# Regrouping VectorE's column copies into loads of 20, 20, 24 and 12 numbers, with destinations fetched for two chunks at a time

## The chip, the cores and the metric

The kernel runs on one core of one Trainium2 chip. The metric is device time in microseconds (us) of one launch; the lower the better. The core has five engines with a queue of instructions each: TensorE (PE, with weight loads shown apart as PEld), VectorE (DVE), ScalarE (ACT), GpSimd (POOL) and SyncE (SP). SP computes nothing here: it loads numbers into registers and issues DMA transfers.

## The reference

One layer of a graph network with 12500 nodes of 48 features and 400000 edges, sorted by destination:

```python
h = jnp.maximum(_layernorm(x, axis=-1), 0.0)
x_i, x_j = h[dst], h[src]
tmp = jnp.concatenate([x_i, x_j, edge_attr], axis=1)   # 48 + 48 + 32
msg = jax.nn.relu(tmp @ W1 + b1) @ W2 + b2             # 128 hidden, then 48
out = x + jax.ops.segment_sum(msg, dst, num_segments=12500)
```

## The kernel before

**Tables.** A first stage of some 100 us (`node_tables`) normalises the nodes and multiplies them by the two node parts of W1. It leaves `tab_a` (for destinations) and `tab_b` (for sources) in HBM, one row of 128 numbers a node, and `bt`, which is `tab_b` turned: 128 partitions by nodes, in SBUF.

**Chunks and tiles.** The stage in question (`windows`) runs over 391 chunks of 1024 edges, each of 8 tiles of 128 edges. Because edges are sorted, the destinations of a chunk lie in a window of 80 nodes. For chunk c:

- SP loads the window's 80 rows of `tab_a` into `rhs` (L474), the edge features into the lower rows of `lhs` (L479), and the chunk's destinations as 16-bit numbers, repeated over 80 partitions, into `row` (L481).
- DVE compares `row` with the window's node numbers and writes the upper 80 rows of `lhs` (L501), and makes `hot`, the same comparison turned (L508).
- PE multiplies `lhs` and `rhs` tile by tile into `pre` in PSUM (`before`, L520). What the sources add comes in one of three ways, below.
- DVE adds `pre` and the fetched rows with the ReLU into `hid` (`gathered`, L540). PE folds `hid` with `hot` into `p_g` (`fold`, L567 and L572), and DVE adds that into the segment being summed (`add`, L586).

**Three ways for the sources.** The rows of `tab_b` for the sources of a tile are

- fetched by POOL with an indirect DMA (L490), 2619 tiles of the 3125;
- or copied column by column out of `bt` into a tile `gt` and added on PE by a product with the identity (`turned`, L530): 458 tiles. Each column is one copy with a register as its address, made by DVE or ACT (`columns`, L431);
- or brought by SP, one line of 512 bytes a DMA (`singles`, L462): 48 tiles, into the buffers `gbs`.

**What sets the order.** The order is written out by hand. The table `PARTS` says how many columns an engine copies at each place in a chunk. Ahead of each group stands one register load of as many numbers (`numbers`, L396, TENSOR_LOAD in the trace); DVE's first group loads one number more, the place used by `add`. Of the 151 columns of a chunk DVE copies 71 and ACT 80. DVE's program of a chunk is: the comparison L501, a load of 24 and 23 copies, `hot` L508, a load of 20 and 20 copies, the sum L540, a load of 20 and 20 copies, the addition L586, a load of 8 and 8 copies. `BYCOLS` spreads the tiles that are copied by columns evenly over the chunks by the total `PART`; `BYROWS` does the same for the tiles that SP brings, by `SINGLE` lines a chunk.

SP's program of a chunk is: a load of one number (the window), three transfers, a load of 16 numbers, 16 lines. `row` has three buffers, `lhs` and `rhs` three each. POOL's fetches for a chunk are issued about seven chunks ahead, each behind a DVE instruction that `paced` chooses, so that they are spread over a chunk.

Of the kernel before, what the change touches and what calls it, by code (L numbers as in the profile page):

```python
# [17 lines left out]
P = 128  # L18
N, D, DE, HID, E = 12500, 48, 32, 128, 400000
# [5 lines left out]
CE = T * P  # L25
# [3 lines left out]
W = 80  # L29
# [18 lines left out]
I16 = mybir.dt.int16  # L48
# [8 lines left out]


PARTS = (
    (True, 0, 23, 1),  # L60
    (True, 23, 20, 24),
    (True, 43, 20, 44),
    (True, 63, 8, 64),
    (False, 71, 16, 72),
    (False, 87, 16, 88),
    (False, 103, 16, 104),
    (False, 119, 16, 120),
    (False, 135, 16, 136),
)
PART = sum(n for _, _, n, _ in PARTS)  # L70
BASE = 152
DVE_PARTS = sum(dve for dve, *_ in PARTS)

BT0 = 16512
SEG0 = 133024
SEG_SIZE = 8 * L


SEG, NEXT, SEG2 = 153, 154, 155
PLACE0 = 156  # L80
SINGLE = 16
SINGLE_AT = 160
WIDTH = 176
SLOTS = (NCH + 2 + P - 1) // P
MOST = 32
HALF_ROWS = 16
# [10 lines left out]
def tiles_of(first, part):  # L97

    n = (END - first) * part // P
    return [first + (P * (j + 1) + part - 1) // part - 1 for j in range(n)]  # L100
# [14 lines left out]
def single_tiles():  # L115

    chunks = []
    for c in tiles_of(COLS, SINGLE):
        c = max(c, chunks[-1] + 1 if chunks else 0)
# [10 lines left out]
def single_at(c):  # L130

    return (0,) if c in BYROWS else ()


def gathered_at(c):

    return [
        t for t in range(min(T, NT - c * T)) if t not in turned_at(c) and t not in single_at(c)
    ]
# [155 lines left out]
def windows(nc, tc, gbs, bt, ident, idx, x_t, tab_a, tab_b, dst, edge_t, w1, w2s, b2s, out_t):  # L295
# [3 lines left out]
    with ExitStack() as es:  # L299
# [1 line left out]

        segs = [seg.tile([P, 2, L], F32, name=f"seg{k}") for k in range(2)]
        one = es.enter_context(tc.tile_pool(name="wone", bufs=1))
        ld = es.enter_context(tc.tile_pool(name="ld", bufs=LOADS))
        gtp = es.enter_context(tc.tile_pool(name="gtp", bufs=8))
        wp = es.enter_context(tc.tile_pool(name="wp", bufs=HIDS))
        ps_p = es.enter_context(tc.tile_pool(name="ps_p", bufs=2, space=PSUM))
# [13 lines left out]
        for _, _, n, at in PARTS:  # L321
# [3 lines left out]
            )  # L325
        rows_at = slice(BASE, BASE + 1)
        singles_at = slice(SINGLE_AT, SINGLE_AT + SINGLE)
        for of in (rows_at, singles_at):
# [5 lines left out]
        for a, b in ((place, SEG2), (NEXT, SEG)):  # L334
# [5 lines left out]
        nc.vector.scalar_tensor_tensor(  # L340
            last[:, :, at_place], last[:, :, at_place], 4.0, last[:, :, PLACE0 : PLACE0 + 1],
            op0=ALU.mult, op1=ALU.add,
# [6 lines left out]
        def after(ins, of, reason):  # L349
            tc.add_manual_dep(  # L350
                ins, of.name,
                mybir.DependencyInfo(
                    mybir.DependencyClass.Sync, mybir.DependencyReason.DATA
                ),
                reason=reason,
            )
# [11 lines left out]
        def buffer(c):  # L368

            if c in BYROWS:  # L370
                return mixed[BYROWS.index(c) % 2]
            k = 0 if len(turned_at(c)) == 1 else 1
            uses[k] += 1
            return gbs[k][(uses[k] - 1) % len(gbs[k])]
# [9 lines left out]
        def group(c):  # L384

            return divmod(c + OFF, GQ)
# [4 lines left out]
        def numbers(c, at, n, engine):  # L391

            got = []
            row, slot = row_of(c)
            for k in range(0, n, MOST):
                got += nc.values_load_multi_w_load_instructions(  # L396
                    last[row : row + 1, slot, at + k : at + min(k + MOST, n)],
                    engines=[engine], min_val=0, max_val=1 << 23,
                    skip_runtime_bounds_check_because="numbers of nodes, and what is made of them",
                )[1]  # L400
            return got
# [6 lines left out]
        def load(c, part):  # L408

            dve, first, n, at = PARTS[part]  # L410
            n = max(0, min(n, len(BYCOLS) * P - ((c - COLS) * PART + first))) if c >= COLS else 0
            engine = mybir.EngineType.DVE if dve else mybir.EngineType.Activation
            if part == 0 and 2 <= c < NCH + 2:
                base, *nodes = numbers(c, at - 1, n + 1, engine)
                st[c - 2]["base"] = base
            else:
                nodes = numbers(c, at, n, engine) if n else []
            regs[c, part] = nodes

        def columns(c, part):  # L420

            dve, first, _, _ = PARTS[part]
            copy = nc.vector.tensor_copy if dve else nc.scalar.copy
            for k, at in enumerate(regs.pop((c, part), [])):
                of, e = divmod((c - COLS) * PART + first + k, P)
                if of not in gts:
                    gts[of] = gtp.tile([HID, P], F32, name="gt")
                at = at.with_bounds(
                    min_val=BT0, max_val=BT0 + 4 * (N - 1), guaranteed_mod_val=0, out_of_modulus=4
                ) - BT0  # L430
                done = copy(gts[of][:, e : e + 1], bt8[:, bass.ds(at, 4)].bitcast(F32))  # L431
                if dve:
                    mark(done, 0.06)
# [4 lines left out]
        def mark(ins, us):  # L438
            marks.append((ins, us))

        def paced(c, j, of):

            span = spans.get(c - AHEAD + 1)
            if j == 0 or not span:
                return None
            upto = sum(us for _, us in span) * j / of
            for ins, us in span:
                upto -= us
                if upto <= 0:
                    return ins  # L450
            return None
# [3 lines left out]
        def singles(c):  # L455

            n = max(0, min(SINGLE, len(BYROWS) * P - (c - COLS) * SINGLE)) if c >= COLS else 0
            for k, row in enumerate(numbers(c, SINGLE_AT, n, mybir.EngineType.SP) if n else ()):
                of, e = divmod((c - COLS) * SINGLE + k, P)
                to = mixed[of % 2][:, single_at(BYROWS[of])[0], :]  # L460
# [4 lines left out]
                )  # L465
                moves.setdefault(BYROWS[of], []).append(moved.ins)

        def prepare(c):
            n = min(T, NT - c * T)
            at = c * CE  # L470
            base, = numbers(c, BASE, 1, mybir.EngineType.SP)
            rhs = rhss[c % 3]
            base = base.with_bounds(min_val=0, max_val=4 * HID * (N - 1))
            nc.sync.dma_start(  # L474
                rhs.bitcast(U8)[:W, :],
                taba8[bass.ds(base, 4 * HID * W)].rearrange("(w h) -> w h", w=W),
            )
            lhs = lhss[c % LOADS]
            nc.sync.dma_start(lhs[W:K, : n * P], edge_t[:, at : at + n * P])  # L479
            row = ld.tile([W, CE], I16, name="row")  # L480
            nc.sync.dma_start(  # L481
                row[:, : n * P],
                dst[at : at + n * P].rearrange("(o e) -> o e", o=1).to_broadcast([W, n * P]),
            )
            st[c] = dict(n=n)
            gb = buffer(c)
            fetched = gathered_at(c)
            fetches = []
            for j, t in enumerate(fetched):
                fetch = nc.gpsimd.indirect_dma_start(  # L490
                    out=gb[:, t, :], out_offset=None, in_=tab_b[:, :],
                    in_offset=bass.IndirectOffsetOnAxis(
                        ap=srci[:, c * T + t : c * T + t + 1], axis=0
                    ),
                )
                fetches.append(fetch.ins)
                behind = paced(c, j, len(fetched))
                if behind is not None:
                    after(fetch.ins, behind.ins, "fetches are spread over a chunk")

            mark(nc.vector.tensor_tensor(  # L501
                lhs[:W, : n * P], row[:, : n * P],
                firsts[:, c : c + 1].to_broadcast([W, n * P]), op=ALU.is_equal,
            ), 1.1)
            load(c, 0)
            columns(c, 0)
            hot = wp.tile([P, T, W], F32, name="hot")
            mark(nc.vector.tensor_tensor(  # L508
                hot[:, :n, :], wnum.unsqueeze(1).to_broadcast([P, n, W]),
                rel[:, c * T : c * T + n].unsqueeze(2).to_broadcast([P, n, W]), op=ALU.is_equal,  # L510
            ), 0.85)
            st[c].update(rhs=rhs, lhs=lhs, gb=gb, hot=hot, fetches=fetches)
# [64 lines left out]
        def add(c):  # L577

            s = st.pop(c)
            k = group(c)[0] % 2  # L580
            of = SEG0 + k * SEG_SIZE
            at = s["base"].with_bounds(
# [45 lines left out]
        with tc.manual_schedule():  # L628
            for c in range(NCH + 2):
                if c < NCH:  # L630
                    prepare(c)
                    singles(c)
# [173 lines left out]
def tile_gnn_preln(  # L806
# [52 lines left out]
    flag = const.tile([1, 1], I32, name="flag")  # L859
    last = const.tile([P, LAST, WIDTH], I32, name="last")  # L860

# [167 lines left out]
```

## Time and profile before

| | |
|---|---|
| median of 3 runs | 3493.72 us (3492.07 to 3495.51) |
| the profiled execution: time | 3493.84 us |
| the profiled execution: span from first to last instruction | 3492.1 us |
| busy: DVE, ACT | 3136.6 us (90%), 3172.3 us (91%) |
| busy: PE, POOL | 2656.1 us (76%), 2493.5 us (71%) |
| granted TensorE clock | 0.776 |
| DMA | 98 GB/s over the span |

Busy time of an engine counts its computing instructions alone: register loads and the issue of DMAs aren't in it, so SP has no busy share at all, and a gap on DVE may be a register load. In the rows below, "[idle before <-releaser]" is the time an engine stood still just before the row and what ended it; "issue" means nothing that the trace shows. SPq and DVEq are the sequencers of SP and DVE.

### The profile page before, as it was taken

The page shows a single profiled execution, that of the slowest core. Times are in us where ns is not written, and L with a number is a line of the kernel's source. Part 1 is how long each engine was busy: PE and PEld are TensorE (multiplying, and loading weights), DVE is VectorE, ACT ScalarE, POOL GpSimd, SP SyncE. Part 2 cuts the span into 40 slices and gives each one's busy share as a digit, 9 for nine tenths or more (in the row PEclk, how much of TensorE's full clock was granted, in tenths as well). Part 3 has the DMA queues.
Part 4 walks back from the last instruction along what each step waited for, and adds up shares of the span by engine and source line. Part 5 has one row for each costly group of instructions (what it writes and reads, how often), then busy time and mean ns, then how long its engine had stood idle before and what let it go on. Part 6 is the DMA issues. An engine that isn't in the chain of part 4 may idle for free.

```text
span 3492.1 us, 121785 instructions
## 1 busy us (share of the span) xinstructions
PE 2656.1 (76%) x17111; PEld 2384.2 (68%) x17111; DVE 3136.6 (90%) x29346; ACT 3172.3 (91%) x31179; POOL 2493.5 (71%) x2656
## 2 busy tenths in 40 slices
PE   8577777777778777777777777777778777777777
PEld 6566666666667667676676677666677676667666
DVE  6799999999999999999999999999999999999997
ACT  5999999998999999998999899999999899989893
POOL 5777777777777777777777777777777777777772
PEclk9777777877777777778777777778777777777777
DMA  5533333333333333333333333333333333333332
GB/s 196 168 98 97 95 97 94 97 98 100 96 96 98 96 96 97 95 97 100 96 97 97 97 95 97 95 98 98 98 96 96 97 95 97 97 96 97 96 99 56
DMA packets 199941, 349.44 MB, mean 100 GB/s; under 512 B 69106, under 2 KB 107396, under 8 KB 197844
## 3 DMA queue, kind: packets, MB, share of 16 engines
q0 software_dynamic: 83840, 171.83, 19.4%
q1 hardware_dynamic: 115024, 169.63, 16.1%
q14 instruction: 672, 5.51, 0.5%
q8 instruction: 145, 2.38, 0.3%
q10 hardware_dynamic: 260, 0.10, 0.0%
HBM read 321.82 MB, written 22.07 MB: 98 GB/s over the span
## 4 chain that ended last, share of the span: by engine, by line
DVE 49%; SPq 16%; PE 9%; ACT 9%; DMA 7%; issue 7%; DVEq 3%; ACTq 1%
DVE gt L431 27%; SPq L462 9%; ACT gt L431 8%; DVE lhs L501 8%; DVE hid L540 7%; DMA row<-in_dst 6%; DVE hot L508 5%; SPq L396 4%; DVEq L396 3%; PE p_g L567 3%; PE pre L520 2%; DVE seg L586 1%; PE p_n L241 1%; SPq L479 1%; SPq L474 1%
## 5 line engine op out<-in xcount | busy, mean ns | idle before, releaser
L431 ACT COPY gt<-bt 128x1 f32 x31040 | 3069.6, 187 | 70.0 <-issue 48.2
L490 POOL DMA_INDIRECT gb<-tab_b,srci x1855 | 1750.1, 943 | 669.2 <-issue 379.6
L431 DVE COPY gt<-bt 128x1 f32 x27584 | 1815.8, 144 | 208.9 <-issue 166.4
L567 PE MATMUL p_g<-hot,hid 128*128 128x80 f32 x6250 | 1075.9, 344 | 695.8 <-DVE hid L540 681.4
L567 PEld LDWEIGHTS p_g<-hot,hid 128*128 128x128 f32 x6250 | 1008.4, 253 | 766.6 <-DVE hid L540 751.1
L520 PEld LDWEIGHTS pre<-rhs,lhs 112*128 112x128 f32 x6250 | 974.1, 245 | 199.6 <-issue 127.9
L520 PE MATMUL pre<-rhs,lhs 112*128 112x128 f32 x6250 | 1013.7, 330 | 111.9 <-PE pre L530 48.7
L490 POOL DMA_INDIRECT gbl<-tab_b,srci x476 | 448.9, 943 | 165.6 <-issue 97.9
L501 DVE TENSOR_TENSOR lhs<-row,compared 80x1024 f32<-80x1024 int16 x391 | 472.5, 1209 | 73.7 <-DMA row<-in_dst 71.9
L490 POOL DMA_INDIRECT gbs<-tab_b,srci x288 | 271.7, 943 | 93.6 <-issue 59.8
L540 DVE CUSTOM_DVE_ANT_0 hid<-pre,gb 128x1024 f32<-128x1024 f32 x275 | 333.3, 1212 | 3.6 <-PE pre L530 3.0
L508 DVE TENSOR_TENSOR hot<-compared,rel 128x640 f32<-128x640 f32 x391 | 318.1, 813 | 0.0
L530 PE MATMUL pre<-ident,gt 128*128 128x128 f32 x916 | 274.8, 408 | 5.3 <-issue 4.8
L572 PE MATMUL p_g<-hot,ones 128*128 128x80 bf16 x3125 | 241.9, 239 | 0.0
L572 PEld LDWEIGHTS <-ones 128*128 128x128 bf16 x3125 | 241.8, 133 | 0.0
L530 PEld LDWEIGHTS pre<-ident,gt 128*128 128x128 f32 x916 | 195.9, 273 | 7.4 <-issue 6.1
L600 ACT COPY seg<-nothing 128x944 f32<-128x944 f32 x64 | 62.4, 975 | 151.1 <-PE p_f L616 151.1
L586 DVE TENSOR_TENSOR seg<-seg,p_g 128x160 f32 x391 | 121.2, 310 | 2.2 <-PE p_g L572 2.2
L616 PE MATMUL p_f<-seg,w2s 128*48 128x512 f32 (+1 forms) x134 | 96.4, 812 | 0.8 <-DVE xseg L622 0.8
L540 DVE CUSTOM_DVE_ANT_0 hid<-pre,gbl 128x1024 f32<-128x1024 f32 x68 | 82.6, 1214 | 3.7 <-PE pre L530 3.6
L617 PE MATMUL p_f<-seg,b2s 1*48 1x512 f32 (+1 forms) x134 | 81.5, 691 | 0.0
L617 PEld LDWEIGHTS p_f<-seg,b2s 1*48 1x48 f32 x134 | 11.9, 130 | 78.4 <-issue 77.0
(74 smaller groups left out, 391.4 us busy)
## 6 DMA issues: line engine op xcount, KB each, us to landing
gbs<-tab_b SPq DMA_DIRECT2D x6144, 0.5 KB
row<-in_dst SPq DMA_DIRECT2D x390, 160.0 KB
lhs<-in_edge_t SPq DMA_DIRECT2D x390, 128.0 KB
gb<-tab_b,srci POOLq DMA_INDIRECT x1855
rhs<-tab_a SPq DMA_DIRECT2D x391, 40.0 KB
gbl<-tab_b,srci POOLq DMA_INDIRECT x476
xseg<-in_x_t SPq DMA_DIRECT2D x33, 192.0 KB
out_x<-xseg SPq DMA_DIRECT2D x33, 192.0 KB
```

Of the source, the lines that this page charges most:

```text
L396: got += nc.values_load_multi_w_load_instructions(last[row : row + 1, slot, at + k : at + min(k + MOST, n)], engines=[engine], min_val=0, ...
L431: done = copy(gts[of][:, e : e + 1], bt8[:, bass.ds(at, 4)].bitcast(F32))
L462: moved = nc.sync.dma_start(to.bitcast(U8)[e : e + 1, :], tabb8[bass.ds(row, 4 * HID)].rearrange("(o h) -> o h", o=1),)
L490: fetch = nc.gpsimd.indirect_dma_start(out=gb[:, t, :], out_offset=None, in_=tab_b[:, :], in_offset=bass.IndirectOffsetOnAxis(ap=srci[:, c ...
L501: mark(nc.vector.tensor_tensor(lhs[:W, : n * P], row[:, : n * P], firsts[:, c : c + 1].to_broadcast([W, n * P]), op=ALU.is_equal,), 1.1)
L508: mark(nc.vector.tensor_tensor(hot[:, :n, :], wnum.unsqueeze(1).to_broadcast([P, n, W]), rel[:, c * T : c * T + n].unsqueeze(2).to_broadca ...
L520: s["behind"] = nc.tensor.matmul(pre[:, t, :], s["lhs"][:K, t * P : (t + 1) * P], s["rhs"][:K, :], start=True, stop=t not in turned_at(c), ...
L530: s["behind"] = nc.tensor.matmul(s["pre"][:, t, :], gts.pop(j), ident, start=False, stop=True).ins
L540: return nc.vector._custom_dve(dve_ops.TENSOR_ADD_SAT, out=to, in0=a, in1=b, s0=float("inf"), s1=0.0)
L567: nc.tensor.matmul(p_g[:, 0, :], s["h"][:, t, :], s["hot"][:, t, :], start=t == 0, stop=t == n - 1)
L572: nc.tensor.matmul(p_g[:, 1, :], ones, high[:, t, 1::2], start=t == 0, stop=t == n - 1)
L586: mark(nc.vector.tensor_add(to, to, s["p_g"]), 0.25)
```

## The change

Three things change. DVE's groups are of 19, 20, 24 and 12 columns in place of 23, 20, 20 and 8: 75 in place of 71, with loads of 20 (19 and the place), 20, 24 and 12 numbers. The total `PART` becomes 155, so that 471 tiles are copied by columns. SP brings 13 lines a chunk in place of 16, 39 tiles in place of 48; POOL fetches 2615 tiles. And the destinations come by one transfer for two chunks, into two buffers of twice the size. The columns behind the numbers of `PARTS` move up by four in the table of numbers, and the segments in SBUF by 128 bytes.

```diff
 PARTS = (
-    (True, 0, 23, 1),
-    (True, 23, 20, 24),
-    (True, 43, 20, 44),
-    (True, 63, 8, 64),
-    (False, 71, 16, 72),
+    (True, 0, 19, 1),
+    (True, 19, 20, 20),
+    (True, 39, 24, 40),
+    (True, 63, 12, 64),
+    (False, 75, 16, 76),
...
-SINGLE = 16
+SINGLE = 13
...
-        ld = es.enter_context(tc.tile_pool(name="ld", bufs=LOADS))
+        ld = es.enter_context(tc.tile_pool(name="ld", bufs=2))
...
-            row = ld.tile([W, CE], I16, name="row")
-            nc.sync.dma_start(
-                row[:, : n * P],
-                dst[at : at + n * P].rearrange("(o e) -> o e", o=1).to_broadcast([W, n * P]),
-            )
+            if c % 2 == 0:
+                pair[0] = ld.tile([W, 2 * CE], I16, name="row")
+                both = min(2 * CE, E - at)
+                nc.sync.dma_start(
+                    pair[0][:, :both],
+                    dst[at : at + both].rearrange("(o e) -> o e", o=1).to_broadcast([W, both]),
+                )
+            row = pair[0][:, c % 2 * CE :]
```

From here on the lines of the changed kernel stand five further down (the comparison L501 is L506 there, the sum L540 is L545, the addition L586 is L591).

DVE's program from the sum of one chunk to the second group of the next stands before so:

```order
L540 ISA hid_732<-pre,gb_0_91 128x1024
L396 TENSOR_LOAD last
L431 COPY gt<-bt 128x1 x20
L586 TENSOR_TENSOR seg_678<-seg_678,p_g 128x2x80
L396 TENSOR_LOAD last
L431 COPY gt<-bt 128x1 x8
L501 TENSOR_TENSOR lhs_728<-row,compared 80x1024
L396 TENSOR_LOAD last
L431 COPY gt<-bt 128x1 x23
L508 TENSOR_TENSOR hot<-compared,rel 128x640
L396 TENSOR_LOAD last
L431 COPY gt<-bt 128x1 x20
```

and in the changed kernel, at such a place, so:

```order
L545 ISA hid_731<-pre,gbs_735 128x1024
L396 TENSOR_LOAD last
L431 COPY gt<-bt 128x1 x24
L591 TENSOR_TENSOR seg_678<-seg_678,p_g 128x2x80
L396 TENSOR_LOAD last
L431 COPY gt<-bt 128x1 x12
L506 TENSOR_TENSOR lhs_730<-row,compared 80x1024
L396 TENSOR_LOAD last
L431 COPY gt<-bt 128x1 x19
L513 TENSOR_TENSOR hot<-compared,rel 128x640
L396 TENSOR_LOAD last
L431 COPY gt<-bt 128x1 x20
```

The five instructions that aren't copies keep their order; four columns leave the group behind the comparison, and four each join the group behind the sum and the one behind the addition.

SP's program of one chunk and a half stands before so (`gbs` takes the single lines):

```order
L396 TENSOR_LOAD last
L474 DMA rhs_746<-tab_a 80x512
L479 DMA lhs_730<-in_edge_t 32x1024
L481 DMA row<-in_dst 80x1024
L396 TENSOR_LOAD last
L462 DMA gbs_734<-tab_b 1x512 x16
L396 TENSOR_LOAD last
L474 DMA rhs_742<-tab_a 80x512
L479 DMA lhs_728<-in_edge_t 32x1024
L481 DMA row<-in_dst 80x1024
```

and in the changed kernel, over two chunks, so:

```order
L396 TENSOR_LOAD last
L476 DMA rhs_746<-tab_a 80x512
L481 DMA lhs_730<-in_edge_t 32x1024
L396 TENSOR_LOAD last
L462 DMA gbs_735<-tab_b 1x512 x13
L396 TENSOR_LOAD last
L476 DMA rhs_742<-tab_a 80x512
L481 DMA lhs_728<-in_edge_t 32x1024
L485 DMA row<-in_dst 80x2048
L396 TENSOR_LOAD last
L462 DMA gbs_735<-tab_b 1x512 x13
```

Only every second chunk has a transfer into `row`, twice as wide, and each chunk has three lines fewer.

More of the change, by code (lines that the diff above doesn't have):

```diff
@@ L59 @@
 PARTS = (
-    (True, 0, 23, 1),
-    (True, 23, 20, 24),
-    (True, 43, 20, 44),
-    (True, 63, 8, 64),
-    (False, 71, 16, 72),
[L65 to L68, printed above, removed]
+    (True, 0, 19, 1),
[3 more added lines that the diff above has]
+    (False, 75, 16, 76),
+    (False, 91, 16, 92),
+    (False, 107, 16, 108),
+    (False, 123, 16, 124),
+    (False, 139, 16, 140),
 )
 PART = sum(n for _, _, n, _ in PARTS)
-BASE = 152
+BASE = 156
 DVE_PARTS = sum(dve for dve, *_ in PARTS)
 BT0 = 16512
-SEG0 = 133024
+SEG0 = 133152
 SEG_SIZE = 8 * L
-SEG, NEXT, SEG2 = 153, 154, 155
-PLACE0 = 156
-SINGLE = 16
-SINGLE_AT = 160
-WIDTH = 176
+SEG, NEXT, SEG2 = 157, 158, 159
+PLACE0 = 160
+SINGLE = 13
+SINGLE_AT = 164
+WIDTH = 180
 SLOTS = (NCH + 2 + P - 1) // P
@@ L466, in singles @@
                 moves.setdefault(BYROWS[of], []).append(moved.ins)
+        pair = [None]
         def prepare(c):
```

## The prediction

> **What bounds the kernel now.** I read the page first: the shares, the chain that ended last, the costly groups; then the waits; then one stretch of the timeline, chunk by chunk; last the register loads.
>
> ```profile
> PE 2656.1 (76%) x17111; PEld 2384.2 (68%) x17111; DVE 3136.6 (90%) x29346; ACT 3172.3 (91%) x31179; POOL 2493.5 (71%) x2656
> ...
> DVE 49%; SPq 16%; PE 9%; ACT 9%; DMA 7%; issue 7%; DVEq 3%; ACTq 1%
> ...
> L431 ACT COPY gt<-bt 128x1 f32 x31040 | 3069.6, 187 | 70.0 <-issue 48.2
> L490 POOL DMA_INDIRECT gb<-tab_b,srci x1855 | 1750.1, 943 | 669.2 <-issue 379.6
> L431 DVE COPY gt<-bt 128x1 f32 x27584 | 1815.8, 144 | 208.9 <-issue 166.4
> ```
>
> No engine is full. DVE has half of the chain and SP's sequencer, which computes nothing, a sixth. The waits, longest first, tell how the two meet (columns: engine, line, what ended the wait, us in all, times, longest):
>
> ```profile
> DVE gt L431 <- issue: 166.4, 478, 1.1
> ACT seg L600 <- PE p_f L616: 151.1, 31, 8.5
> DVE lhs L501 <- DMA row<-in_dst: 71.9, 88, 7.5
> ...
> DVE hid L540 <- PE pre L530: 7.8, 9, 1.6
> ```
>
> DVE loses 72 us to the transfer into `row`, next to nothing to PE, and 166 us to "issue" ahead of column copies. How SP spends a chunk, from its own timeline (start, length):
>
> ```profile
> 1509.68 0.32 SPq L474 DMA_DIRECT2D rhs<-tab_a  x1
> 1510.05 0.42 SPq L479 DMA_DIRECT2D lhs<-in_edge_t  x1
> 1510.56 0.38 SPq L481 DMA_DIRECT2D row<-in_dst  x1
> 1512.09 5.16 SPq L462 DMA_DIRECT2D gbs<-tab_b  x16
> 1517.99 0.32 SPq L474 DMA_DIRECT2D rhs<-tab_a  x1
> ```
>
> From one `rhs` to the next are 8.31 us without a pause for anyone: 5.16 us are the 16 lines (0.323 us each), the rest three transfers and two register loads. A chunk takes on average
>
> ```profile
> L501 DVE TENSOR_TENSOR lhs<-row,compared x391: 808/1208/1218, 106.8 to 3470.4; 80x1024 f32<-80x1024 int16 x195, 80x640 f32<-80x640 int16 x1
> ```
>
> (3470.4 - 106.8) / 390 = 8.62 us. SP with its segment transfers on top is almost as slow as that, so it has no reserve: it issued `row` at 1510.56, and the comparison that needs it stands at 1514.20, 3.6 us later. Now the same stretch on DVE:
>
> ```profile
> 1505.98 1.21 DVE L501 TENSOR_TENSOR lhs<-row,compared 80x1024 f32<-80x1024 int16 x1
> 1507.55 1.49 DVE L431 COPY gt<-bt 128x1 f32 x23 [0.36 <-issue]
> 1508.95 0.81 DVE L508 TENSOR_TENSOR hot<-compared,rel 128x640 f32<-128x640 f32 x1
> 1509.85 1.30 DVE L431 COPY gt<-bt 128x1 f32 x20
> 1511.07 1.21 DVE L540 CUSTOM_DVE_ANT_0 hid<-pre,gb 128x1024 f32<-128x1024 f32 x1
> 1512.20 1.29 DVE L431 COPY gt<-bt 128x1 f32 x20
> 1513.41 0.31 DVE L586 TENSOR_TENSOR seg<-seg,p_g 128x160 f32 x1
> 1513.71 0.58 DVE L431 COPY gt<-bt 128x1 f32 x8
> 1514.20 1.21 DVE L501 TENSOR_TENSOR lhs<-row,compared 80x1024 f32<-80x1024 int16 x1
> 1515.68 1.49 DVE L431 COPY gt<-bt 128x1 f32 x23 [0.27 <-issue]
> 1517.09 0.81 DVE L508 TENSOR_TENSOR hot<-compared,rel 128x640 f32<-128x640 f32 x1
> ...
> 1522.13 0.30 DVE L586 TENSOR_TENSOR seg<-seg,p_g 128x160 f32 x1
> 1522.36 0.56 DVE L431 COPY gt<-bt 128x1 f32 x8
> 1522.84 1.20 DVE L501 TENSOR_TENSOR lhs<-row,compared 80x1024 f32<-80x1024 int16 x1
> 1524.22 1.48 DVE L431 COPY gt<-bt 128x1 f32 x23 [0.18 <-issue]
> ```
>
> The holes stand behind the comparison, ahead of the 23 copies: 0.36, 0.27 and 0.18 us. Behind the sum L540 there is none: the 20 copies start 0.08 us before the sum's recorded end (1511.07 + 1.21 against 1512.20). What fills the holes is the register load; four single ones on DVE (length three times, then the start) and two on SP:
>
> ```profile
> L396 DVEq TENSOR_LOAD <-last x1: 1601/1601/1601, 1522.5 to 1522.5; - x1
> L396 DVEq TENSOR_LOAD <-last x1: 1357/1357/1357, 1510.5 to 1510.5; - x1
> L396 DVEq TENSOR_LOAD <-last x1: 1348/1348/1348, 1516.5 to 1516.5; - x1
> L396 DVEq TENSOR_LOAD <-last x1: 599/599/599, 1521.6 to 1521.6; - x1
> ...
> L396 SPq TENSOR_LOAD <-last x1: 979/979/979, 1511.0 to 1511.0; - x1
> L396 SPq TENSOR_LOAD <-last x1: 538/538/538, 1517.3 to 1517.3; - x1
> ```
>
> On DVE 24 numbers take 1.60 us, 20 take 1.35, 8 take 0.60: 0.063 us a number. A load starts while its engine still works off what is queued: the one at 1510.5 began some 0.55 us, nine copies, before the sum behind which it stands in the program, and so was over (1511.9) before the sum was. The load of 24 began only 0.3 us before its comparison at 1522.84, because just 8 copies are between it and the load before; it ended at 1524.1, and 0.09 us later came the first copy. So the bound is DVE's program with its loads, held up at times by SP.
>
> **The change part by part**, against the profiled execution (3493.84 us, of which 1.7 lie around the span; the median of the runs is 0.1 us less).
>
> *Four more columns.* The copies on DVE become 29,175: 471 tiles of 128 columns less ACT's 31,113. That is 1,591 more, each at the pitch of a running group, (1.49 - 0.14) / 22 = 0.061 us: **+98 us**, all on the path. ACT makes 73 more, 7 us, beside its 151 us of waiting.
>
> *SP.* Three lines fewer save 0.97 us, 13 numbers for 16 save 3/15 of the 0.44 us between its two loads, 0.09, and half a `row` saves some 0.2 (0.42 from its issue to the load at 1511.0). SP then needs 7.05 us of DVE's 8.5, and runs ahead until `rhs` and `lhs`, three buffers each, stop it. The wait for `row` should go: **-72 us**, at the worst 0. The transfer is twice as big; if landing took twice the 3.6 us, a lead of 7.2 us would be needed, and three buffers give more: the product of chunk c-3 frees them nearly two chunks, 11 us, before the comparison of chunk c. What is late next is DVE itself.
>
> *20 numbers in place of 24 behind the comparison.* The load is 0.25 us shorter, it has 12 copies before it rather than 8, and no wait of the comparison keeps it back. It then lies as the load of 20 behind the sum does, with no hole. The three rows show holes of 0.27 us on average; the 166.4 us of "issue" over 391 chunks, less 0.1 behind L508 (1508.95 + 0.81 to 1509.85), give 0.33. With the 0.08 that a hidden load gains that is 0.35 to 0.41; I take 0.38 x 389 = **-148 us** (bounds -97, the shorter load alone, and -160).
>
> *12 numbers in place of 8 behind the addition.* 0.25 us longer. The load of 8 ends at 1522.2, the copies start at 1522.36; less the 0.09 us from load to copy, 0.07 us are spare. So 0.18 us shows, x 389 = **+70 us** (bounds 0 and the whole 0.25, +97).
>
> *24 numbers in place of 20 behind the sum.* The load began at 1510.5; with 1.60 us and 0.09 it allows a copy at 1512.2, just where the first one stands now: 0 to 0.03 us a chunk. Behind L508, with 19 copies ahead rather than 23, I allow 0.01. Together **+13 us**, at the worst +97.
>
> *POOL.* Its fetches follow at 0.943 us plus a gap of 379.6 / 1244 = 0.305 us:
>
> ```profile
> POOL gb L490 <- issue: 379.6, 1244, 0.5
> ```
>
> 2615 of them, 6.69 a chunk, need 8.34 us a chunk. It is the next bound: below 8.34 us a chunk, at about 3384 us in all, DVE would find rows missing. The forecast of 8.52 stays above it.
>
> Sum: 98 - 72 - 148 + 70 + 13 = -39 us, 3455 us (-1.1%).
>
> **The rivals.**
> - *The load of 12 costs no more than the load of 8.* Then the +70 goes: **3385 us**, at POOL's bound, 0.17 together with whatever lies between it and the forecast. For it: the load begins beside copies and an addition. Against it: 8, 20 and 24 numbers lie on one line. The Trainium skill, page "DMA: Bandwidth & Descriptors", section Latency and other measured facts, has a floor of about 600 ns for a register load, by which 8 and 12 numbers might cost the same; the loads of 20 and 24 above grow with the count, and no row here shows a floor for 12.
> - *Nothing gained.* DVE, earlier at the sum, meets PE there, and half of the 72 us comes back as that wait: 98 - 36 - 148 + 70 + 13 = -3, **3491 us**, 0.10. Only 7.8 us of such waits stand in the profile, which speaks against more.
> - *Slower: the hole moves.* The 24 numbers now stand behind the sum. If the sum has to wait there, for PE or for rows, its load starts only with it, as behind the comparison at 1505.98 (0.36 us of hole). The whole 0.25 us then shows behind the sum and behind the addition, +84 and +27 on the forecast: **3566 us**, 0.11. It decides from the point where the load starts less than 0.5 us before the sum; the row shows 0.55.
> - *Slower by little: the load starts seven copies ahead of the sum, not nine.* The cover is then 2 x 0.061 = 0.12 us shorter, x 389 = +47: **3502 us**, 0.04. For it speaks only that the 0.55 us is one reading. The Trainium skill, page "Advanced Engine Details and Errata", section Engine Queue Depths, gives VectorE a queue of 8 instructions, which would be seven copies and the sum; the load at 1510.5, nine copies ahead, doesn't agree.
>
> **How the numbers follow.** The forecast, between 3420 and 3487, has 0.58. A measurement of this kernel can tell 0.2%, 7 us, from no change. Faster by more than that: 0.58 + 0.17 = 0.75; within it 0.10; slower 0.15. The range reaches down to 3400, into the first rival, and up to 3510, past the fourth: about 0.1 is left out at either end, the first rival at its full price and the third at its.
>
> **What would show it.** In the changed profile the wait of the comparison for `row` is near 0, and SP shows pauses ahead of `rhs`. The first copy stands 1.13 us behind the comparison's start, 0.4 us behind the addition's (0.23 before), 1.13 to 1.16 behind the sum's. "issue" ahead of DVE's copies falls to some 100 us and lies behind L586 and L508 of the old numbering. POOL's gaps beyond 0.305 us shrink. I am wrong if the comparison still waits, if holes stand behind the sum, or if DVE waits for PE or for rows at the sum.

## The result, and the profile after

The changed kernel takes 3447.94 us (median of 4 runs, 3445.11 to 3449.59) where the kernel before takes 3492.89: a ratio of 0.9874, 95% interval 0.9856 to 0.9892. The forecast was 3455. The profiled execution took 3449.59 us with a span of 3447.9.

The page of the changed kernel, its shares, its chain and the groups that answer to those of before:

```profile
PE 2687.3 (78%) x17137; PEld 2369.3 (69%) x17137; DVE 3236.5 (94%) x30937; ACT 3178.9 (92%) x31252; POOL 2496.5 (72%) x2652
...
DVE 85%; PE 4%; DVEq 4%; issue 4%
...
L495 POOL DMA_INDIRECT gb<-tab_b,srci x1919 | 1815.3, 946 | 659.8 <-issue 404.6
L431 DVE COPY gt<-bt 128x1 f32 x29175 | 1919.4, 143 | 128.1 <-issue 66.1
...
L506 DVE TENSOR_TENSOR lhs<-row,compared 80x1024 f32<-80x1024 int16 x391 | 471.2, 1205 | 7.1 <-DMA row<-in_dst 7.1
```

SP's sequencer had 16% of the chain and is gone from it; DVE has 85% in place of 49%. The balance on DVE is plain: it works 100 us more (3236.5 against 3136.6) and stands still 144 us less (3447.9 - 3236.5 = 211.4 against 355.5). The difference, 44 us, is the change of the span.

SP's waits, from the view of waits of the changed kernel's SP queue (what ended the wait, us, times, longest), show an engine with time to spare:

```profile
SPq L631 <- DVE xseg L627: 292.1, 32, 29.9
SPq L476 <- PE pre L525: 127.0, 43, 8.9
```

Before, the same two waits were 28.7 and 21.1 us. SP now stands ahead of `rhs` until PE is done with it, as the prediction said, and ahead of the store of a segment. DVE's timeline of two chunks:

```profile
1509.61 0.82 DVE L431 COPY gt<-bt 128x1 f32 x12
1510.35 1.20 DVE L506 TENSOR_TENSOR lhs<-row,compared 80x1024 f32<-80x1024 int16 x1
1511.48 1.23 DVE L431 COPY gt<-bt 128x1 f32 x19
...
1515.34 1.21 DVE L545 CUSTOM_DVE_ANT_0 hid<-pre,gb 128x1024 f32<-128x1024 f32 x1
1516.47 1.53 DVE L431 COPY gt<-bt 128x1 f32 x24
1517.92 0.30 DVE L591 TENSOR_TENSOR seg<-seg,p_g 128x160 f32 x1
1518.32 0.82 DVE L431 COPY gt<-bt 128x1 f32 x12
1519.06 1.21 DVE L506 TENSOR_TENSOR lhs<-row,compared 80x1024 f32<-80x1024 int16 x1
1520.18 1.23 DVE L431 COPY gt<-bt 128x1 f32 x19
```

Behind the comparison the first copy stands 1.13 us later, without a hole; behind the sum 1.13; behind the addition 0.40, where 0.23 stood before. The load of 12 is the reason for the last:

```profile
L396 DVEq TENSOR_LOAD <-last x1: 851/851/851, 1517.4 to 1517.4; - x1
```

It takes 0.85 us and ends at 1518.25, past the start of the addition it stands behind.

### The profile page after: what moved, and what is told of

It is laid out like the page before. It is cut to its first block, busy times and chain, and to the rows that moved or that the text cites. A ratio compares the mean times of both kernels' runs of the same rounds, so it can differ in the third digit from the quotient of the medians.

```text
span 3447.9 us, 120765 instructions
## 1 busy us (share of the span) xinstructions
PE 2687.3 (78%) x17137; PEld 2369.3 (69%) x17137; DVE 3236.5 (94%) x30937; ACT 3178.9 (92%) x31252; POOL 2496.5 (72%) x2652
## 3 DMA queue, kind: packets, MB, share of 16 engines
q0 software_dynamic: 83712, 171.57, 19.7%
## 4 chain that ended last, share of the span: by engine, by line
DVE 85%; PE 4%; DVEq 4%; issue 4%
DVE gt L431 50%; DVE hid L545 12%; DVE lhs L506 12%; DVE hot L513 8%; DVEq L396 4%; DVE seg L591 2%; PE p_g L572 2%; DVE xseg L627 1%; PE pre L525 1%; PE p_f L621 0%; PE p_f L622 0%; PE pre L535 0%; PE p_g L577 0%; DVE seg L611 0%; DVEq L611 0%
## 5 line engine op out<-in xcount | busy, mean ns | idle before, releaser
L495 POOL DMA_INDIRECT gb<-tab_b,srci x1919 | 1815.3, 946 | 659.8 <-issue 404.6
L431 DVE COPY gt<-bt 128x1 f32 x29175 | 1919.4, 143 | 128.1 <-issue 66.1
L572 PE MATMUL p_g<-hot,hid 128*128 128x80 f32 x6250 | 1039.1, 336 | 541.8 <-DVE hid L545 531.3
L572 PEld LDWEIGHTS p_g<-hot,hid 128*128 128x128 f32 x6250 | 976.9, 246 | 609.2 <-DVE hid L545 597.4
L525 PE MATMUL pre<-rhs,lhs 112*128 112x128 f32 x6250 | 1036.0, 335 | 150.7 <-PE pre L535 70.8
L495 POOL DMA_INDIRECT gbl<-tab_b,srci x462 | 437.1, 946 | 151.8 <-issue 91.0
L506 DVE TENSOR_TENSOR lhs<-row,compared 80x1024 f32<-80x1024 int16 x391 | 471.2, 1205 | 7.1 <-DMA row<-in_dst 7.1
L545 DVE CUSTOM_DVE_ANT_0 hid<-pre,gb 128x1024 f32<-128x1024 f32 (+1 forms) x286 | 346.8, 1213 | 1.9 <-PE pre L535 1.2
L495 POOL DMA_INDIRECT gbs<-tab_b,srci x234 | 221.4, 946 | 79.7 <-issue 46.7
L591 DVE TENSOR_TENSOR seg<-seg,p_g 128x160 f32 x391 | 121.3, 310 | 2.2 <-PE p_g L577 2.2
L621 PE MATMUL p_f<-seg,w2s 128*48 128x512 f32 (+1 forms) x134 | 109.2, 911 | 0.8 <-DVE xseg L627 0.8
L622 PE MATMUL p_f<-seg,b2s 1*48 1x512 f32 (+1 forms) x134 | 97.3, 815 | 0.0
L545 DVE CUSTOM_DVE_ANT_0 hid<-pre,gbl 128x1024 f32<-128x1024 f32 x66 | 80.1, 1214 | 0.6 <-PE pre L535 0.6
```

Source lines behind the costliest of these rows:

```text
L495: fetch = nc.gpsimd.indirect_dma_start(out=gb[:, t, :], out_offset=None, in_=tab_b[:, :], in_offset=bass.IndirectOffsetOnAxis(ap=srci[:, c ...
L506: mark(nc.vector.tensor_tensor(lhs[:W, : n * P], row[:, : n * P], firsts[:, c : c + 1].to_broadcast([W, n * P]), op=ALU.is_equal,), 1.1)
L525: s["behind"] = nc.tensor.matmul(pre[:, t, :], s["lhs"][:K, t * P : (t + 1) * P], s["rhs"][:K, :], start=True, stop=t not in turned_at(c), ...
L545: return nc.vector._custom_dve(dve_ops.TENSOR_ADD_SAT, out=to, in0=a, in1=b, s0=float("inf"), s1=0.0)
L572: nc.tensor.matmul(p_g[:, 0, :], s["h"][:, t, :], s["hot"][:, t, :], start=t == 0, stop=t == n - 1)
L591: mark(nc.vector.tensor_add(to, to, s["p_g"]), 0.25)
```

## The experiments

Every kernel is the changed one with the edit shown. The diffs of `PARTS` show DVE's rows alone; ACT's five groups of 16 follow on them. Times are medians; the ratio is to the kernel before on the same chip, and for its interval 95% is meant.

For the terms of the prediction one measure is used in all of them: the distance from the start of a DVE instruction to the start of the next copy, averaged over all chunks of the trace between 200 and 3400 us where a copy follows directly, in us. In the 31 chunks where the copy of a segment stands behind the addition, the last column counts from that copy. The first column is the distance from the last copy to the comparison, 0.06 where it doesn't wait.

| | ahead of the comparison | behind it | behind L508 | behind the sum | behind the addition |
|---|---|---|---|---|---|
| before | 0.255 | 1.572 | 0.931 | 1.167 | 0.231 |
| changed | 0.061 | 1.154 | 0.939 | 1.212 | 0.397 |
| SP's part alone | 0.061 | 1.445 | 0.925 | 1.154 | 0.229 |
| the groups alone | 0.125 | 1.203 | 0.945 | 1.218 | 0.400 |
| 24 numbers back behind the comparison | 0.061 | 1.384 | 0.932 | 1.147 | 0.393 |

### SP's part alone

```diff
-    (True, 0, 19, 1),
-    (True, 19, 20, 20),
-    (True, 39, 24, 40),
-    (True, 63, 12, 64),
+    (True, 0, 23, 1),
+    (True, 23, 20, 24),
+    (True, 43, 20, 44),
+    (True, 63, 8, 64),
```

Expected:

> SP's part of the change alone: 13 lines a chunk and one transfer of destinations for two chunks, with DVE's groups as before (23, 20, 20 and 8 columns); POOL has 13 tiles more than in the changed kernel (2628). Theory (SP's wait and the place of the loads are separate terms): the wait of the comparison for row is near 0; first copies stand 1.4 us behind the comparison (1.15 in the changed kernel) and 0.23 behind the addition; DVE needs about 8.3 us a chunk, less than POOL's 8.4, so POOL sets the end and the time is 3400 us (3385 to 3425). Rival one (POOL is no bound): 3448 - 0.22 x 389 = 3362 us. Rival two (the regrouping is the main gain): the hole of 148 us comes back on the changed kernel, less 98 + 70 for the columns and the load that are gone: about 3430 us or more, with POOL idle as before.

Measured: 3354.63 us, ratio 0.9601 (0.9585 to 0.9617): 93 us faster than the whole change. Its page with the chain that ended last, the first and last fetch from the view of POOL's line, DVE's wait at the sum, and the comparison in an early and a late stretch (times, then first and last start):

```profile
PE 2573.1 (77%) x17111; PEld 2300.9 (69%) x17111; DVE 3123.7 (93%) x29346; ACT 3170.9 (95%) x31179; POOL 2503.3 (75%) x2665
...
DVE 66%; ACT 20%; issue 4%; DVEq 3%; PE 2%; ACTq 1%; DMA 0%; SPq 0%
...
L506 DVE TENSOR_TENSOR lhs<-row,compared 80x1024 f32<-80x1024 int16 x391 | 471.2, 1205 | 8.2 <-DMA row<-in_dst 8.2
...
L495 POOL DMA_INDIRECT gb<-tab_b,srci x1904: 940/944/1367, 51.1 to 3331.7; - x191
...
DVE hid L545 <- PE pre L535: 3.7, 5, 1.1
...
L506 DVE TENSOR_TENSOR lhs<-row,compared x203: 1197/1206/1218, 119.6 to 1793.8; 80x1024 f32<-80x1024 int16 x102
...
L506 DVE TENSOR_TENSOR lhs<-row,compared x161: 1199/1206/1219, 2000.4 to 3325.4; 80x1024 f32<-80x1024 int16 x161
```

The wait for `row` is gone as in the changed kernel, and the holes of the 24 numbers are still there (1.445 us behind the comparison). POOL issues from 51.1 to 3331.7 us without one longer pause but the first: apart from the 19.7 us for `tab_b` at the start, it never stands still for more than 0.32 us. 2628 fetches in 3281 us are 1.248 us each, 8.39 a chunk.

And yet POOL doesn't set this kernel's time. It has no share in the chain, DVE waits 3.7 us in all for PE at the sum, and a chunk of DVE takes 8.29 us early and 8.28 late ((1793.8 - 119.6) / 202 and (3325.4 - 2000.4) / 160). POOL, at 8.39, is slower than that, but it starts with a lead, the time from the start of a chunk's last fetch to the chunk's sum (the fetches counted off in order in the trace):

| lead of the fetches, us | chunk 25 | chunk 200 | chunk 300 | chunk 375 |
|---|---|---|---|---|
| changed | 57 | 59 | 58 | 58 |
| SP's part alone | 53 | 35 | 24 | 16 |
| fewer columns (below) | 51 | 13 | 4 | 5 |

Losing 0.1 us a chunk, POOL uses up its lead only at the very end: 16 us are left at chunk 385 and 5 at the last, as much as in the kernel with fewer columns where DVE waits. So the theory has both paces right, 8.3 us for DVE and 8.4 for POOL, but it doesn't count the lead; the time is DVE's own, and rival one, at 3362, is right to 7 us. A faster DVE would gain nothing here, as the run with fewer columns shows. ACT has little in reserve too: its waits ahead of the clearing of a segment have fallen from 151.1 to 16.8 us.

### The groups alone

```diff
-SINGLE = 13
+SINGLE = 16
...
-        ld = es.enter_context(tc.tile_pool(name="ld", bufs=2))
+        ld = es.enter_context(tc.tile_pool(name="ld", bufs=LOADS))
...
-            if c % 2 == 0:
-                pair[0] = ld.tile([W, 2 * CE], I16, name="row")
...
+            row = ld.tile([W, CE], I16, name="row")
+            nc.sync.dma_start(
+                row[:, : n * P],
...
```

Expected:

> DVE's groups of 19, 20, 24 and 12 columns alone; SP as before, with 16 lines and one transfer into row a chunk. Theory (SP has no reserve): the comparison waits for row again, 40 to 100 us in all, its load starts late in those chunks, and the time is 3480 to 3510 us. Rival (SP's wait was only what a late DVE made of it): under 20 us of waits and 3440 to 3455 us, as the changed kernel.

Measured: 3506.36 us, ratio 1.0042 (1.0028 to 1.0056). Two rows of DVE's waits:

```profile
DVE gt L431 <- issue: 83.0, 257, 3.2
DVE lhs L501 <- DMA row<-in_dst: 26.9, 33, 6.1
```

The time is in the theory's range; the waits for `row`, 27 us, are less than the 40 to 100 that it expected, and 20 us more than in the changed kernel. The hole behind the comparison has shrunk without SP's help (1.203 against 1.572 us), and yet nothing is gained: the 1591 copies and the load of 12 take it back. So the groups by themselves cost 13 us, and the whole gain of the change is SP's.

### Fewer columns

```diff
-    (True, 63, 12, 64),
+    (True, 63, 8, 64),
```

Expected:

> The changed kernel with 8 columns in the last group in place of 12 (71 in all, 13 tiles more for POOL, 2628). Theory (DVE's program is what sets the changed kernel's time, POOL comes next): DVE needs 0.25 us less for the columns and 0.17 less for the load a chunk, 8.1 us, which POOL with 8.4 can't follow; the time is POOL's, 3400 us (3380 to 3425), the same as with SP's part alone, and DVE waits for PE or rows at the sum by 0.2 us a chunk or more. Rival (POOL keeps up): 3448 - 0.42 x 389 = 3285 us. Rival two (DVE isn't the bound of the changed kernel): 3440 us or more.

Measured: 3355.82 us, ratio 0.9606 (0.959 to 0.9622), the same as SP's part alone within 1.2 us, though DVE's program is shorter: behind the comparison a copy stands 1.191 us away by the same measure (1.445). One wait of DVE and the one of PE behind it, the comparison in the early and the late stretch, and POOL's line:

```profile
DVE hid L545 <- PE pre L535: 41.6, 33, 4.4
...
PE pre L535 <- DMA gb<-tab_b,srci: 88.3, 44, 4.3
...
L506 DVE TENSOR_TENSOR lhs<-row,compared x206: 1198/1206/1218, 119.2 to 1795.4; 80x1024 f32<-80x1024 int16 x103
...
L506 DVE TENSOR_TENSOR lhs<-row,compared x158: 812/1206/1218, 2006.6 to 3322.6; 80x1024 f32<-80x1024 int16 x157, 80x640 f32<-80x640 int16 x1
...
L495 POOL DMA_INDIRECT gb<-tab_b,srci x1904: 940/944/1386, 50.8 to 3331.1; - x191
```

Here POOL does become the bound, but only in the second half. Early a chunk takes 8.18 us (1676.2 / 205); by chunk 225 the lead is down to 5 us, and from then on a chunk takes 8.38 (1316.0 / 157), which is POOL's pace. DVE, shortened, waits 42 us at the sum for PE's product, which in turn waits for fetched rows. POOL's last fetch stands at 3331.1, at 3331.7 in the other: it is the end that no faster DVE can beat with 2628 fetches, 3355 us and not the 3400 of the theory. That SP's part alone ends within 1.2 us of it is chance; there DVE just about uses the lead up. DVE's wait at the sum, 0.11 us a chunk, is half of what the theory expected.

Four columns less with a load of 8 in place of 12 save 92 us in all. Early, while the rows are there, they save 0.36 us a chunk (8.18 against 8.54 in the changed kernel over the same stretch) of the 0.42 expected. So DVE's program is what sets the changed kernel's time, and rival two falls.

### The 24 numbers back behind the comparison

```diff
-    (True, 0, 19, 1),
-    (True, 19, 20, 20),
-    (True, 39, 24, 40),
+    (True, 0, 23, 1),
+    (True, 23, 20, 24),
+    (True, 43, 20, 44),
```

Expected:

> The changed kernel with the 24 numbers back behind the comparison: groups of 23, 20, 20 and 12 columns, 75 in all, SP and POOL as in the changed kernel. Theory (a load is hidden by what is queued ahead of it, so its place counts): first copies 1.35 to 1.45 us behind the comparison in place of 1.15, 1.13 behind the sum in place of 1.18: +0.15 to +0.25 us a chunk, 3505 to 3545 us. Rival (the holes came from the waiting comparison, not from the length of the load): 3440 to 3460 us.

Measured: 3508.39 us, ratio 1.0046 (1.0029 to 1.0063), 60 us over the changed kernel, with the same columns, lines and fetches. DVE's timeline:

```profile
1507.76 1.20 DVE L506 TENSOR_TENSOR lhs<-row,compared 80x1024 f32<-80x1024 int16 x1
1509.13 1.48 DVE L431 COPY gt<-bt 128x1 f32 x23 [0.17 <-issue]
```

The copies stand 1.37 us behind a comparison that waited for nothing. By the table the place of the four numbers is worth 0.230 us a chunk behind the comparison less 0.065 behind the sum, 0.165 x 389 = 64 us. A load's price depends on what is queued ahead of it.

### More lines, and no pair: two chips that say little

The pair is the one transfer of destinations for two chunks.

```diff
-SINGLE = 13
+SINGLE = 16
```

> The changed kernel with 16 lines a chunk in place of 13; one transfer of destinations for two chunks stays, DVE's groups stay (POOL has 9 tiles fewer). Theory (SP needs only to be clearly under DVE's 8.5 us a chunk): SP needs 7.05 + 1.06 = 8.1 us and some 0.2 for the segments, waits for row stay under 20 us, 3440 to 3465 us. Rival (the lines are what makes row late, as in the run with the groups alone): waits of 25 us or more, 3475 to 3510 us.

and, with 13 lines, the transfer into `row` once a chunk as in the diff of the groups alone:

> The changed kernel with one transfer of destinations a chunk, as before, into three buffers; 13 lines and DVE's groups stay. Theory: SP needs 7.25 us a chunk, the wait for row is under 10 us, 3440 to 3455 us: the pair is worth nothing here. Rival (the pair is what brings row early, since its second half is there a chunk ahead): waits of 25 us or more and 3470 us or more.

> The changed kernel with one transfer of destinations a chunk, into three buffers, once more for the same reason. Theory (13 lines alone give SP its reserve): wait for row under 10 us, 3440 to 3455 us where the kernel before takes 3493. Rival (the pair is what brings row early): waits of 25 us or more and 3470 us or more.

Measured: 4481.37 us with 16 lines, ratio 0.9904 (0.987 to 0.9939); 4476.57 and 4538.22 us without the pair, ratios 0.9896 (0.9862 to 0.993) and 0.9874 (0.9851 to 0.9898). The kernel before took 4527 and 4591 us on these two chips. DVE's timeline of the kernel with 16 lines, and ACT's of the same moments:

```profile
1501.87 0.21 DVE L431 COPY gt<-bt 128x1 f32 x2 [0.50 <-issue]
1502.63 0.15 DVE L431 COPY gt<-bt 128x1 f32 x1 [0.54 <-issue]
1503.33 0.70 DVE L431 COPY gt<-bt 128x1 f32 x10 [0.55 <-issue]
...
1501.88 0.28 ACT L431 COPY gt<-bt 128x1 f32 x2 [0.44 <-issue]
1502.63 0.19 ACT L431 COPY gt<-bt 128x1 f32 x1 [0.46 <-issue]
1503.33 6.06 ACT L431 COPY gt<-bt 128x1 f32 x61 [0.51 <-issue]
```

Both engines stand still for half a microsecond and start again at the same instants, in the middle of groups where nothing is awaited. With chunks 30% longer, SP and POOL have time in any case, so neither theory is tested. The waits for `row` were 7.2 us without the pair, but that is no evidence for an undisturbed chip. What the pair alone is worth stays open.

### 73 columns and 15 lines

```diff
-    (True, 63, 12, 64),
+    (True, 63, 10, 64),
...
-SINGLE = 13
+SINGLE = 15
```

> Groups of 19, 20, 24 and 10 columns (73), 15 lines, one transfer of destinations for two chunks; POOL has 2616 tiles, 12 fewer than the two kernels that it bounded at 3355 us. Theory (POOL's fetches set the end, 1.249 us each): 3355 - 12 x 1.249 = 3340 us (3330 to 3350), with no gaps on POOL beyond 0.305 us. Rival (DVE, with two columns more than 71 and a load of 10, becomes the bound): half way to the changed kernel, 3385 to 3420 us, and POOL has gaps again.

> The kernel with groups of 19, 20, 24 and 10 columns, 15 lines and one transfer of destinations for two chunks once more, since the chip of its first run held every engine up (the kernel before took 4527 us there). Theory (POOL's fetches set the end): 3340 us (3330 to 3350) where the kernel before takes 3493, no gaps on POOL beyond 0.305 us. Rival (DVE becomes the bound): 3385 to 3420 us, with gaps on POOL. If the kernel before is far from 3493 us again, the run says nothing of either.

> The kernel with groups of 19, 20, 24 and 10 columns, 15 lines and one transfer of destinations for two chunks a third time, since both chips that ran it so far held every engine up. Theory (POOL's fetches set the end): 3340 us (3330 to 3350) where the kernel before takes 3493, no gaps on POOL beyond 0.305 us. Rival (DVE becomes the bound): 3385 to 3420 us, with gaps on POOL. If the kernel before is far from 3493 us again, the run says nothing of either.

Measured: on the two chips above 4456.01 and 4521.7 us, ratios 0.9852 (0.9813 to 0.9891) and 0.9854 (0.9825 to 0.9883). On a third chip, where the kernel before took 3493.96: 3500.11 us, ratio 1.0021 (1.0011 to 1.0031). Both expectations miss (and of the two kernels at 3355 us from which they start, POOL bounds only the one with fewer columns): with two columns fewer than the changed kernel it is 52 us slower. DVE's timeline and one register load of that run:

```profile
1514.31 0.31 DVE L591 TENSOR_TENSOR seg<-seg,p_g 128x160 f32 x1
1514.95 0.70 DVE L431 COPY gt<-bt 128x1 f32 x10 [0.34 <-issue]
...
L396 DVEq TENSOR_LOAD <-last x1: 1080/1080/1080, 1513.8 to 1513.8; - x1
```

The load of 10 numbers takes 1.08 us, more than one of 12 (0.85). A load goes by fours: 8, 12, 20 and 24 numbers lie on a line of 0.25 us for four, and each number left over costs about as much as four, 2 x 0.24 on the 0.60 of eight. Behind the addition the mean distance is 0.605 us, 0.208 more than in the changed kernel, x 389 = 81 us, of which 823 copies fewer give 50 back; behind the comparison it is 0.041 longer (1.195), 16 us. That is 47 of the 52 us. SP's load of 15 takes 1.38 us, 0.4 more than one of 13 (0.97), for two more numbers left over.

A kernel with 9 columns and 16 lines ran once, on the first of the disturbed chips, and has the same fault, a load of 9:

> Groups of 19, 20, 24 and 9 columns (72), 16 lines, one transfer of destinations for two chunks; POOL has 2616 tiles as in the kernel with 73 columns and 15 lines. Theory (POOL sets the end): 3340 us (3330 to 3350), the same as that one. Rival one (SP at 8.1 us a chunk and some 0.2 for the segments is as slow as POOL's 8.35): the comparison waits for row, 3355 to 3390 us. Rival two (DVE bounds the one with 73 columns): this one is faster than that by 0.1 us a chunk, 40 us.

It took 4453.28 us, ratio 0.9834 (0.9799 to 0.9869), and says nothing of the bound for the same reason.

### 71 columns and 16 lines

```diff
-    (True, 63, 12, 64),
+    (True, 63, 8, 64),
...
-SINGLE = 13
+SINGLE = 16
```

> Groups of 19, 20, 24 and 8 columns (71), 16 lines, one transfer of destinations for two chunks: every load of DVE and the load of SP's lines has a multiple of four numbers; POOL has 2619 tiles, 9 fewer than the two kernels at 3355 us. Theory (POOL's fetches set the end there): 3355 - 9 x 1.249 = 3344 us (3335 to 3352) where the kernel before takes 3493, no gaps on POOL beyond 0.305 us. Rival (SP, at 7.1 + 3 x 0.323 us a chunk and some 0.2 for the segments, is as slow as POOL's 8.36 us): the comparison waits for row by 20 us or more and the time is 3360 to 3400 us.

Measured: 3437.86 us, ratio 0.984 (0.9826 to 0.9853). The rival has the cause right, SP, but the time lies above its range too. The longest wait of DVE, and SP's timeline:

```profile
DVE lhs L506 <- DMA row<-in_dst: 109.3, 87, 7.4
...
1506.60 5.50 SPq L462 DMA_DIRECT2D gbs<-tab_b  x16
1512.86 0.32 SPq L476 DMA_DIRECT2D rhs<-tab_a  x1
1513.23 0.42 SPq L481 DMA_DIRECT2D lhs<-in_edge_t  x1
1513.75 0.36 SPq L485 DMA_DIRECT2D row<-in_dst  x1
1515.25 5.15 SPq L462 DMA_DIRECT2D gbs<-tab_b  x16
1521.29 0.35 SPq L631 DMA_DIRECT2D out_x<-xseg  x1
1522.34 0.33 SPq L476 DMA_DIRECT2D rhs<-tab_a  x1
```

From the first line of one chunk to that of the next SP takes 8.65 us here, with `row` between, and a chunk with the store of a segment takes 9.5 from `rhs` to `rhs`; POOL needs 8.36, and DVE, with the same groups, took 8.18 early in the kernel with fewer columns. That kernel differs by the three lines a chunk alone (and the 9 tiles that POOL fetches for them); beside it the three lines cost 82 us. So for this program of DVE the pair without the three lines isn't enough. Whether the lines would be enough without the pair stays open.

## Why the prediction was right, point by point

The sum was right, 39 us forecast and 45 measured by the medians, and so were its mechanisms; the misses of single terms, 15 us at the most, cancel in part. By its own terms:

- *Four more columns*, +98: 1591 more copies, and the copies' busy time grows from 1815.8 to 1919.4 us, +104.
- *The wait for `row`*, -72: 71.9 us have become 7.1 in the view of waits; the distance ahead of the comparison falls by 0.194 us, x 389 = -75. That SP needs some 7 us a chunk was right (6.84 us at the least from one `rhs` to the next without `row`, 7.32 with it), but its load of 13 numbers saves nothing against one of 16 (0.974 against 0.979 us), since it goes by fours; 0.09 us of the step were wrong. The last run shows that with 71 columns the pair without the three lines doesn't carry this term; what each of the two is worth with 75 isn't shown.
- *The hole behind the comparison*, -148: 1.572 to 1.154 us, x 389 = -163. The step named three causes and priced one, the shorter load, at 97. By the table the comparison that no longer waits is worth 0.127 us a chunk, 49 us (before against SP's part alone); 12 copies ahead of it in place of 8 are worth 0.061, 24 us (SP's part alone against the 24 numbers back); and the shorter load 0.230, 89 us (that run against the changed kernel).
- *12 numbers behind the addition*, +70: 0.231 to 0.397 us, +65. The line through 8, 20 and 24 gave 0.85 us for the load, and 0.851 was measured; that line is true for multiples of four alone, which the step didn't know.
- *24 numbers behind the sum*, with L508, +13: 0.045 and 0.008 us, +21.

With 98 for the columns these are -54 us against 44 of the span. Most of the 10 us between lie at a place that no term covers: ahead of the copy of a segment (L611), behind the same load of 12, DVE waits 21.3 us in place of 9.5.

Of the rivals, the one in which the load of 12 costs no more than one of 8 is refuted by the 0.851 us. The slower one, in which the sum waits for PE, had its condition missing: DVE's wait for PE there is some 2 us in the changed kernel, which also refutes the one that gains nothing. The one in which the load starts seven copies ahead had 47 us; 18 are measured behind the sum, and the load of 24 starts 0.55 us, nine copies, ahead of it in the median chunk. Two signs came out otherwise than written: "issue" ahead of DVE's copies fell to 66 us and not to 100, and behind the sum the mean is 1.21 us, above the 1.13 to 1.16.

What the rivals didn't have is that a part of the change is worth more than the whole: the forecast put SP's term and the groups' term side by side as if each were owed to the change, and didn't ask what SP's part alone gives. By its own numbers that was 72 us and a part of the 148; measured are 139 us for SP's part alone. The table finds 75 of them ahead of the comparison and 49 behind it, where the comparison no longer holds its load back, and 7 behind L508 and the sum. The groups give 93 us back, once SP no longer holds DVE up.

The prediction's bound for POOL was mis-sized as well. It put 3384 us, for 2615 fetches, by taking the chunk's 8.34 us and leaving the rest as it stood. A slower POOL first uses up its lead of seven chunks, and only then holds DVE up: in the kernel before 63 us pass from the start of the last fetch (3429.1) to the end of the span, in the kernel with fewer columns 23 (3331.1 to 3353.7). Those 40 us let the kernel with 2628 fetches end at 3355.8, below the 3384 that were put for 2615.

The version that beats both kernels is the smaller one: 13 lines a chunk and one transfer of destinations for two chunks, with DVE's groups left as they were, 3354.63 us or 0.9601 of before.

## What to carry to other kernels

When a change has two parts, price each alone against the profile: here one part was worth 4% and the other took two thirds of it back, and the sum still looked like a success. A slower engine that starts with a lead is no bound until the lead is gone, so compare the lead early and late, and not only the two paces. An engine that only issues transfers has no busy share; measure from one of its loops to the next whether it has a reserve. A stall of a register load is a matter of what is queued ahead of it, so give the long load to the place behind the long instruction, count its numbers in fours, and don't add numbers where the cover is short.

## What the runs showed of the hardware that wasn't expected

- A register load goes by fours: on DVE 8, 12, 20 and 24 numbers take 0.60, 0.85, 1.35 and 1.60 us, 10 take 1.08; on SP 13 and 16 take 0.97 and 0.98 us, 15 take 1.38.
- Behind a comparison that waits for a transfer the load doesn't start before the comparison does (0.01 us after it in the kernel before); behind one that needn't wait it starts earlier, in the changed kernel by 0.34 us in the median (behind the sum by 0.55). In the run of 71 columns and 16 lines the copies stand 1.48 us behind a comparison that waited (97 chunks, in which it starts over 0.1 us after the last copy) and 1.21 behind one that didn't.
- POOL's indirect fetches of 128 rows follow each other every 1.248 us, 0.944 of them recorded as busy, for some 3280 us on end. In the kernel with fewer columns that is the bound, from the chunk at which the lead is used up, and POOL shows 75% busy.
- On two chips DVE and ACT stood still together for half a microsecond at a time, and the kernel before took 30% longer there. In the kernel with 16 lines waits on nothing that the trace shows add up to 759 us ahead of DVE's copies and 910 ahead of ACT's; in the changed kernel, on an undisturbed chip, they are 66 and 47. What holds them up isn't known.
